# Writing the ranks into the first table with two half-size transfers, from SyncE and from ScalarE

## The chip, the cores and the metric

The kernel runs on one core of one Trainium2 chip. Times are device microseconds of that core. The kernel before took 3037.67 us (median of 3 runs, 3028.95 to 3050.73).

## What is computed

Four graph-attention layers run over one graph of 3327 nodes with 512 features a node. The adjacency is symmetric, has ones on its diagonal and is sparse (two nodes are joined with a probability of about 0.0048). Each layer normalises the rows, cuts them at zero, projects them, weighs the neighbours of each node by a softmax over them, and adds the mean to its input:

```python
h = jnp.maximum(_layernorm(x, axis=-1), 0.0)
x = x + layer(h, adj)                      # four times: 8, 4, 1 and 8 heads

# inside a layer, for each head
v = h @ W                                  # features
e = leaky_relu(s_target[:, None] + s_source[None, :], 0.2)
e = where(adj > 0, e, -inf)
out = softmax(e, axis=1) @ v               # elu after layers 1 and 2
```

## The kernel before

The nodes are padded to 3328 and cut into 26 tiles of 128 rows. There are two stages.

**First stage (`tile_gat_stack`, from L543).** For each tile of adjacency rows, GpSimd multiplies the row by descending keys (L695) and VectorE takes the largest 40 of them (L704, L659 to L661). That gives each node the list of its neighbours, in `L`. Beside this, the first layer's features are computed on TensorE, and for each node a row of 1056 numbers goes to the table `tabx` in DRAM (`features`, L684, on SyncE's queue): the features and scores of the source in the first half of the row, the node's own x and scores in the second. The rows of x come in on ScalarE's queue (L723).

The nodes are then ranked by the length of their lists, so that the 26 tiles of the second stage hold nodes with lists of like length (`CAPS` gives the length of each tile). `held` is the length of each node's list; `sorted_in` and `placed` count how many nodes come earlier. L735 to L739 add this up to `rank`, a tile of 128 x 26 numbers: column t holds the ranks of the nodes of tile t. From `rank` two things are made:

- L741 writes it to `tabx`, one number to each of the 3328 rows, in column `F // 2` = 256. It is one transfer on SyncE's queue. A node that gathers a neighbour's row so gets the neighbour's rank with it.
- L744 to L747 split it into `hi` (the tile) and `lo` (the place in the tile). With these, VectorE makes two sets of 0/1 masks and list copies (L765 to L782), and TensorE sorts the lists by rank by multiplying with the masks (L786). ScalarE copies the result to index tiles (L787, and doubled at L788), in two parts: part a holds the lists of tiles 18 to 25, part b those of tiles 1 to 17 and of tile 0.

One value, `bad`, tells whether the lists fit; the engines load it at L790 and branch. With these inputs the branch goes to `tile_gat_lists`.

**Second stage (`tile_gat_lists`, from L796).** The four layers go through the tiles in the order 25 to 0. For each tile, groups of up to four neighbours are fetched ahead (`fetch`, L857): GpSimd issues one indirect transfer for each neighbour (L835), which gathers 128 rows by one column of an index tile. In layer 0 it gathers from `tabx`. VectorE and ScalarE make the weights (`scored`, L876), VectorE multiplies (L917), and TensorE adds up (L922). In layer 0, ScalarE also takes the ranks out of the gathered rows (L894) and overwrites the indices with them, since the tables of the later layers (`tab0`, `tab1`) are written in the order of the ranks. Tiles of nodes with many neighbours are computed densely beside this in layers 1 to 3 (`Several`, `Wholes`).

**What sets the order.** Around the edit, GpSimd, TensorE, VectorE and ScalarE keep the order in which the program is written (`manual_schedule`, L732); SyncE's order is the scheduler's. Every engine starts its instructions in its own order. A transfer adds to one of eight completion counters, taken in turn by the transfers of SyncE and ScalarE, and who needs its data waits for that counter. The first gather, issued by GpSimd, so waits for the rows of `tabx`, for the ranks and for the indices.

Of the kernel before, what the change touches and what calls it, by code (L numbers as in the profile page):

```python
# [18 lines left out]
P = 128  # L19
# [505 lines left out]
def tile_gat_stack(ctx: ExitStack, tc: tile.TileContext, x, adj, adjT, ws, avs, out):  # L525
# [10 lines left out]
    nc = tc.nc  # L536
    NP, F = x.shape
    N = adjT.shape[0]
    NT = NP // P
# [5 lines left out]
    tabx = dram.tile([NP + 1, 2 * ROW], F32, name="tabx")  # L545
# [15 lines left out]
    with ExitStack() as c1:  # L561
# [170 lines left out]
        with tc.manual_schedule(engines={mybir.EngineType.Pool, mybir.EngineType.PE,  # L732
                                         mybir.EngineType.DVE, mybir.EngineType.Activation}):

            nc.vector.tensor_tensor_scan(base[:, 1:], ones[:, :BINS], count, 0.0, OP.mult, OP.add)  # L735
            nc.vector.tensor_mul(o, o, base[:, :BINS].unsqueeze(1).to_broadcast([P, NT, BINS]))
            rank = small.tile([P, NT], F32, name="rank", bufs=1)
            nc.vector.tensor_reduce(rank, o, AX.X, OP.add)
            nc.vector.tensor_add(rank, rank, part)  # L739

            nc.sync.dma_start(tabx[:NP, :].rearrange("(t p) c -> p t c", p=P)[:, :, F // 2:F // 2 + 1],  # L741
                              rank.unsqueeze(2))
            hi = small.tile([P, NT], F32, name="hi", bufs=1)
            nc.vector.tensor_scalar(hi, rank, 1.0 / P, -(P - 1) / 2.0 / P, OP.mult, OP.add)  # L744
            nc.vector.tensor_scalar(hi, hi, ROUND, -ROUND, OP.add, OP.add)
            lo = small.tile([P, NT], F32, name="lo", bufs=1)
            nc.vector.scalar_tensor_tensor(lo, hi, -float(P), rank, OP.mult, OP.add)  # L747

            junk = small.tile([P, BINS], F32, name="junk")
            nc.vector.tensor_tensor(junk, base[:, :BINS], limit, OP.is_gt)
            nc.vector.tensor_reduce(wrong[:, 2:3], junk, AX.X, OP.add)
            pn = ps_n.tile([P, BANK], F32, name="pn", bufs=1)
            nc.tensor.matmul(pn[0:1, :3], ones[:, 0:1], wrong, start=True, stop=True)
            worst = small.tile([1, 1], F32, name="worst", bufs=1)
            nc.vector.tensor_reduce(worst, pn[0:1, :3], AX.X, OP.max)
            nc.vector.tensor_copy(bad, worst)


            for i, part_ in enumerate(slots.parts):
                t0, t1 = min(b[0] for b in part_.blocks), max(b[1] for b in part_.blocks)
                high = fixed[:, 304:512] if i == 0 else ps_k.tile([P, BANK], F32, name="high")
                high = high[:, :NT * (t1 - t0)].rearrange("p (t h) -> p t h", h=t1 - t0)
                nc.vector.tensor_tensor(high, ahead[:, t0:t1].unsqueeze(1).to_broadcast([P, NT, t1 - t0]),  # L765
                                        hi.unsqueeze(2).to_broadcast([P, NT, t1 - t0]), OP.is_equal)
                n = part_.columns
                if i == 0:
                    (_, _, k, _), = part_.blocks
                    every = once.tile([P, NT, n], F32, name="every")  # L770
                    nc.vector.tensor_tensor(every.rearrange("p t (h k) -> p t h k", k=k),
                                            L[:, :, :k].unsqueeze(2).to_broadcast([P, NT, t1 - t0, k]),
                                            high.unsqueeze(3).to_broadcast([P, NT, t1 - t0, k]), OP.mult)
                pi = ps_i.tile([P, BANK], F32, name="pi")
                for t in range(NT):
                    if i == 0:
                        rhs = every[:, t, :]
                        nc.vector.tensor_scalar(low[:, t, :], ahead, lo[:, t:t + 1], None, OP.is_equal)
                    else:
                        rhs = spare[:, t % 2, :]  # L780
                        for b0, b1, k, c in part_.blocks:
                            nc.vector.tensor_tensor(  # L782
                                rhs[:, c:c + (b1 - b0) * k].rearrange("p (t k) -> p t k", k=k),
                                L[:, t, :k].unsqueeze(1).to_broadcast([P, b1 - b0, k]),
                                high[:, t, b0 - t0:b1 - t0].unsqueeze(2).to_broadcast([P, b1 - b0, k]), OP.mult)
                    nc.tensor.matmul(pi[:, :n], low[:, t, :], rhs, start=(t == 0), stop=(t == NT - 1))  # L786
                nc.scalar.activation(part_.idx, pi[:, :n], AF.Copy)  # L787
                nc.scalar.activation(part_.twice, pi[:, :n], AF.Copy, scale=2.0)  # L788
# [655 lines left out]
```

## Time and profile before

| | |
|---|---|
| median of 3 runs | 3037.67 us |
| the profiled execution | 2485.15 us |
| its span, first to last instruction | 2483.4 us |
| first stage, to `rank` | 0 to 259 us |
| from `rank` to the first gather | 259 to 273.5 us |
| layers 0 to 3 | 273.5 to 2483.4 us |
| VectorE busy, 0 to 259 / 259 to 273.5 | 215.54 / 13.29 us |
| ScalarE busy, 0 to 259 / 259 to 273.5 | 179.09 / 0.43 us |
| GpSimd busy, 0 to 259 / 259 to 273.5 | 210.26 / 0.04 us |

The profiled execution is one run and shorter by 552.5 us than the median of the others. Times in the views count from the span's start. A row of the timeline gives start, duration, engine, line, operation, what it writes and reads, and in brackets how long its engine had been idle before it and what ended that. "SPq" is the sequencer of SyncE, "POOLq" that of GpSimd; a transfer's row there is its issue, not its movement. The releaser in brackets is inferred.

### The profile page before, as it was taken

The page shows a single profiled execution, that of the slowest core. Times are in us where ns is not written, and L with a number is a line of the kernel's source. Part 1 is how long each engine was busy: PE and PEld are TensorE (multiplying, and loading weights), DVE is VectorE, ACT ScalarE, POOL GpSimd, SP SyncE. Part 2 cuts the span into 40 slices and gives each one's busy share as a digit, 9 for nine tenths or more (in the row PEclk, how much of TensorE's full clock was granted, in tenths as well). Part 3 has the DMA queues.
Part 4 walks back from the last instruction along what each step waited for, and adds up shares of the span by engine and source line. Part 5 has one row for each costly group of instructions (what it writes and reads, how often), then busy time and mean ns, then how long its engine had stood idle before and what let it go on. Part 6 is the DMA issues. An engine that isn't in the chain of part 4 may idle for free. (4 is left out here: it accounts for less than half of the span.)

```text
span 2483.4 us, 26799 instructions
## 1 busy us (share of the span) xinstructions
PE 2077.1 (84%) x6832; PEld 1161.7 (47%) x6832; DVE 1935.1 (78%) x5004; ACT 910.9 (37%) x2506; POOL 1709.5 (69%) x1700
## 2 busy tenths in 40 slices
PE   3778699999988846999999986869696699999897
PEld 1666345454444423555555543444353454455453
DVE  7988787887777725888888867978979488787776
ACT  4777024343321102434333323433333444333330
POOL 7898467777777756776777746655545377777775
PEclk9888899999999977999999998989898899999999
DMA  6796579999987878887888858867776488888885
GB/s 229 300 304 236 174 240 283 298 289 293 275 269 235 232 182 243 263 248 227 247 259 258 253 150 272 268 197 250 209 227 204 141 254 246 247 249 248 242 242 173
DMA packets 262490, 599.55 MB, mean 241 GB/s; under 512 B 103923, under 2 KB 121331, under 8 KB 257974
## 3 DMA queue, kind: packets, MB, share of 16 engines
q0 software_dynamic: 126128, 438.08, 58.6%
q1 hardware_dynamic: 132454, 152.86, 19.1%
q10 hardware_dynamic: 3744, 6.82, 0.8%
q8 instruction: 55, 0.90, 0.1%
q14 instruction: 109, 0.89, 0.1%
HBM read 547.96 MB, written 49.65 MB: 241 GB/s over the span
## 5 line engine op out<-in xcount | busy, mean ns | idle before, releaser
L922 PE MATMUL bank<-m,ident 128*128 128x512 f32 x2608 | 1202.3, 607 | 131.9 <-DVE m L917 131.2
L917 DVE TENSOR_TENSOR m<-g,pw 128x512 f32<-128x512 f32 x1304 | 810.7, 681 | 138.2 <-ACT pw L891 133.2
L835 POOL DMA_INDIRECT g<-tab,idxb x734 | 697.8, 951 | 281.7 <-issue 170.7
L922 PEld LDWEIGHTS bank<-m,ident 128*128 128x128 f32 x2608 | 482.7, 193 | 711.8 <-issue 345.2
L469 PE MATMUL pv<-w,hT 128*128 128x264 f32 x1664 | 439.0, 419 | 71.0 <-ACT hT L458 41.7
L891 ACT ACTIVATE pw<-z 128x32 f32<-128x32 f32 (+5 forms) x434 | 84.0, 194 | 987.8 <-DVE z L890 987.5
L469 PEld LDWEIGHTS pv<-w,hT 128*128 128x128 f32 x1664 | 336.5, 206 | 173.2 <-ACT hT L458 48.3
L835 POOL DMA_INDIRECT g<-tabx,twiceb x342 | 324.0, 947 | 104.4 <-issue 77.1
L835 POOL DMA_INDIRECT g<-tab,idxa x297 | 283.0, 953 | 148.0 <-issue 81.3
L1138 PE MATMUL whole<-ve,em 128*128 128x512 f32 x468 | 222.0, 623 | 41.0 <-DVE em L1124 38.9
L888 DVE TENSOR_TENSOR z<-g,pw 128x32 f32<-128x32 f32 (+5 forms) x434 | 75.0, 173 | 195.8 <-DMA g<-tab,idxa 88.4
L695 POOL TENSOR_TENSOR key<-a,keys 128x3328 int32<-128x3328 int32 (+1 forms) x29 | 189.4, 6536 | 16.6 <-DVE cand L704 12.9
L912 DVE SCALAR_TENSOR_TENSOR bank<-g,pw,bank 128x512 f32<-128x512 f32 x243 | 183.2, 754 | 6.8
L1138 PEld LDWEIGHTS whole<-ve,em 128*128 128x128 f32 x468 | 90.5, 199 | 151.1 <-issue 91.8
L704 DVE MAX8 cand<-key 128x8 f32<-128x208 int32 x416 | 143.8, 364 | 0.1
L835 POOL DMA_INDIRECT g<-tabx,twicea x99 | 94.4, 954 | 69.6 <-issue 31.3
L451 PE MATMUL pt<-ident,xn 128*128 128x128 f32 x416 | 68.8, 292 | 84.5 <-ACT hT L458 30.9
L451 PEld LDWEIGHTS pt<-ident,xn 128*128 128x128 f32 x416 | 54.3, 150 | 121.5 <-issue 49.4
L1113 ACT ACTIVATE r<-low,mc,b 128x384 f32<-128x384 f32 x78 | 52.6, 674 | 150.1 <-DVE em L1124 115.7
L1247 ACT ACTIVATE r<-low,spare 128x256 f32<-128x256 f32 x208 | 98.9, 476 | 5.1
L432 POOL TENSOR_TENSOR rstd<-ve,half 128x1 f32<-128x1 f32 x52 | 31.9, 615 | 94.8 <-DVE ve L975 60.4
L890 DVE SCALAR_TENSOR_TENSOR z<-z 128x32 f32<-128x32 f32 (+5 forms) x434 | 78.7, 181 | 15.2 <-DVE z L888 0.2
(175 smaller groups left out, 2113.6 us busy)
## 6 DMA issues: line engine op xcount, KB each, us to landing
a<-in_adj SPq DMA_DIRECT2D x25, 1664.0 KB
tab<-v SPq DMA_DIRECT2D x78, 264.0 KB
ve<-tab SPq DMA_DIRECT2D x78, 264.0 KB
g<-tab SPq DMA_DIRECT2D x66, 264.0 KB
tabx<-vx SPq DMA_DIRECT2D x26, 528.0 KB
g<-tab,idxb POOLq DMA_INDIRECT x734, 3.9
low<-tab SPq DMA_DIRECT2D x52, 132.0 KB
room<-tab SPq DMA_DIRECT2D x52, 132.0 KB
```

The source lines that it names most:

```text
L451: nc.tensor.transpose(pt[:, k, :], xn[:, k * P:(k + 1) * P], ident)
L469: nc.tensor.matmul(pv[:, s, :HF + 8], hT[:, k, :], W.w[:, k, s, :], start=(k == 0), stop=(k == KC - 1))
L695: nc.gpsimd.tensor_tensor(key[:, c:c + quarter], a[:, c:c + quarter], keys[:, c:c + quarter], OP.mult)
L704: nc.vector.max(cand[:, g * 8:(g + 1) * 8], key[:, g * SEG:(g + 1) * SEG])
L835: nc.gpsimd.indirect_dma_start(out=out_, out_offset=None, in_=table, in_offset=bass.IndirectOffsetOnAxis(ap=which, axis=0))
L890: nc.vector.scalar_tensor_tensor(z, z, SLOPE, z, OP.mult, OP.max)
L891: nc.scalar.activation(self.wt[:, k0:k0 + n, :H], z, AF.Exp)
L912: nc.vector.scalar_tensor_tensor(acc, v, w, acc, OP.mult, OP.add)
L917: nc.vector.tensor_tensor(m[:, q, :].rearrange("p (s h d) -> p s h d", s=2, d=D), v.rearrange("p s (h d) -> p s h d", d=D), wt[:, k0 + q, ...
L922: nc.tensor.matmul(self.po, ident, m[:, q, :], start=(k0 + q == 0), stop=(k0 + q == K - 1))
L1138: nc.tensor.matmul(tl.po.rearrange("p (s m) -> p s m", s=2), e[:, q * P:(q + 1) * P], v.rearrange("p (s m) -> p s m", s=2)[:, :, :F // 2], ...
L1247: nc.scalar.activation(self.r[:, h, :], self.a[:, g, :], AF.Relu, bias=-1.0, scale=self.b[:, j, g:g + 1])
```

## The change

The view of the 3328 places in `tabx` gets a name. The ranks of tiles 0 to 12 are written by a transfer on SyncE's queue, those of tiles 13 to 25 by one on ScalarE's queue. Each is of 128 x 13 numbers in place of 128 x 26. In the program the second stands between the copies of the last list (L630) and those of the first index part (L787 of before). Nothing else is edited. The lines after it move down by one.

```diff
             nc.vector.tensor_reduce(rank, o, AX.X, OP.add)
             nc.vector.tensor_add(rank, rank, part)
 
-            nc.sync.dma_start(tabx[:NP, :].rearrange("(t p) c -> p t c", p=P)[:, :, F // 2:F // 2 + 1],
-                              rank.unsqueeze(2))
+            places = tabx[:NP, :].rearrange("(t p) c -> p t c", p=P)[:, :, F // 2:F // 2 + 1]
+            nc.sync.dma_start(places[:, :NT // 2, :], rank[:, :NT // 2].unsqueeze(2))
+            nc.scalar.dma_start(places[:, NT // 2:, :], rank[:, NT // 2:].unsqueeze(2))
             hi = small.tile([P, NT], F32, name="hi", bufs=1)
             nc.vector.tensor_scalar(hi, rank, 1.0 / P, -(P - 1) / 2.0 / P, OP.mult, OP.add)
```

## The prediction

> **What bounds the kernel now.** I read the page's first part for the whole, then only the stretch in which the edited line runs, because a transfer of 13 KB can only matter where somebody waits for it. The page first:
>
> ```profile
> span 2483.4 us, 26799 instructions
> PE 2077.1 (84%) x6832; PEld 1161.7 (47%) x6832; DVE 1935.1 (78%) x5004; ACT 910.9 (37%) x2506; POOL 1709.5 (69%) x1700
> ```
>
> TensorE is busy for 84% of the span, VectorE for 78%, GpSimd for 69%: over the whole no single engine is the bound. The edited line runs once, at 258.86 us, between the two large stages: before it the edge lists are sorted (VectorE 215.5 us of the first 259.0), after it the four layers run. So the question is local: which wait ends last in front of the first gather, the first instruction that reads what the edited line writes? The timeline from 258 us on, with start, duration, engine, line and the idle time before:
>
> ```profile
> 258.65 0.19 DVE L739 TENSOR_TENSOR rank<-rank,part 128x26 f32<-128x26 f32 x1
> 258.86 0.37 SPq L741 DMA_DIRECT2D tabx<-rank  x1
> ...
> 260.76 3.40 DVE L771 TENSOR_TENSOR every<-L,fixed 128x3120 f32<-128x3120 f32 x1
> 264.08 6.80 DVE L778 TENSOR_SCALAR low<-fixed,lo 128x128 f32<-128x128 f32 x26
> ...
> 264.48 8.08 PE L786 MATMUL pi<-every,low 128*128 128x120 f32 x52 [4.41 <-DVE low L778]
> ...
> 272.59 0.27 ACT L787 ACTIVATE idxa<-pi 128x120 int32<-128x120 f32 x1 [18.34 <-PE pi L786]
> 272.76 0.27 ACT L788 ACTIVATE twicea<-pi 128x120 int32<-128x120 f32 x1
> ...
> 273.46 1.19 POOL L835 DMA_INDIRECT g<-tabx,twicea  x1 [29.15 <-DMA av<-in_a]
> ```
>
> Two branches leave `rank` at 258.84 us. One is the transfer. The other makes the gather's indices: VectorE to 270.88, TensorE to 272.56, ScalarE to 273.03. The gather starts at 273.46, 0.43 us after the index tile is finished, and cannot start earlier whatever the transfer does. The page names a load of `av` as the releaser; that load was issued at 267.27 and the gather neither reads nor overwrites it, so I take the label as an inference from a shared completion counter. GpSimd's own semaphore instructions in front of that gather say the same more directly (durations are min/median/max in ns):
>
> ```profile
> L835 POOLq EVENT_SEMAPHORE  x5: 17/43/6863, 265.4 to 265.7; - x5
> ```
>
> The long one starts at 265.7 and ends 6.863 us later, at 272.56: that is TensorE's end (264.48 + 8.08). Everything else that GpSimd waited for there was already done. When did the transfer land? The DMA view of the queues (packets, MB, share of the 16 engines), cut to 258.5 to 265 us:
>
> ```profile
> q1 hardware_dynamic: 3344, 0.01, 25.7%
> ```
>
> and cut to the one us from 260:
>
> ```profile
> q1 hardware_dynamic: 1701, 0.01, 75.6%
> ```
>
> 3344 packets on SyncE's queue are 26 x 128 = 3328 ranks and 16 more, and in the second us the 16 DMA engines were busy to 75.6%. Cutting the view finer, the first packets come in 259 to 260 us and the last at about 262.24. So the transfer takes 262.24 - 258.86 = 3.4 us, and its cover is 273.46 - 262.24 = 11.2 us.
>
> **What the Trainium skill says.** "DMA: Bandwidth & Descriptors", section "Rules for kernel authors": a DMA whose last dimension is not contiguous becomes one descriptor for each element. The trace agrees (3344 packets for 3328 elements). The same page, "Why a DMA increments its semaphore by 16 and not by 1": each engine in use posts its own completion, 16 for a transfer over 128 partitions; 3344 - 3328 = 16 agrees. The same page, "Issuing engines are not separate DMA queues": transfers started by different engines run on the same 16 DMA engines and interleave, so a second issuer saves only the sequencer's time. The trace of before has no such pair; the 75.6% says that little is left to gain. "Perfetto Trace Analysis", "DMA Instruction — HWDGE (DVE, Sync)": the profiled window of such an instruction is its issue, not the movement; 0.37 us against 3.4 us agrees.
>
> **The change part by part.**
>
> *SyncE's issue, now of 13 tiles.* One issue of 0.37 us stays, for 1664 elements in place of 3328. If it shrinks with the number, it saves up to 0.19 us. SyncE then loads the branch flag at 260.5 and next issues at 265.71, in the other branch. Worth 0.
>
> *ScalarE's issue, added.* The row to price it by is ScalarE's loads of x (L723): 334 ns median, 957 ns at most. In the built program it stands behind L630, which starts at 254.01 and lasts 0.24, and ahead of L787 at 272.59; it waits for `rank` (258.84) and for five DMA counters of earlier row writes. Before, SyncE's issue waited for those same five counters, and it started 0.02 us after `rank`, so they are no later. It should start near 258.9 and end before 259.9. Behind it on ScalarE are L787 and L788, on which the gather waits, and they wait for TensorE until 272.56: 12.7 us of ScalarE's idle time (18.34 in all) cover an issue of 0.33 to 0.96. Worth 0; without that cover up to 1 us.
>
> *The movement.* 3328 data packets stay and completions go from 16 to 32: 3360 packets. From 1701 packets in one us, 16 more cost about 0.01 us. If the two queues fill the engines from 75.6% to 100%, the 3344 packets, which take some 2.5 us of movement, end 0.6 us sooner. If the queues do not overlap at all, the second half starts after the first: a second 0.8 us of latency between issue and first packet (258.86 to about 259.7), so 0.8 us later. The landing moves between -0.8 (with the saved issue) and +0.8 us, and I take -0.3. All of it is under the 11.2 us of cover, so the value for the end is 0 at both ends. With the cover gone it would be that same -0.8 to +0.8.
>
> *Waits.* The first gather has one counter more to wait for. GpSimd's semaphore instructions there take 17 ns at least and 43 at the median, and they run from 265.4, ahead of the long wait for TensorE: 0, without cover 0.05. Every later transfer of SyncE and ScalarE moves on by one of eight completion counters. I compared the built orders: PE, DVE and GpSimd issue the same instructions in the same order, ScalarE has one more, SyncE's later order is the same, and once counters are renumbered, the waits in the layers that run are unchanged but for one additional one at the first products of layer 0 (VectorE L917, at 302.20) and one fewer on ScalarE's copy of x; the additional one is for a transfer landed 40 us before. Worth 0.
>
> Sum: 0 + 0 + 0 + 0 = 0 us against the profiled execution, 2485.15 us (span 2483.4 and 1.75 around it). The runs shown have a median of 3037.67, 552.5 us more than the profiled execution; this profile does not show where that goes, so I carry the sum over as it is: 3037.7 us. For the transfer to matter in those runs, it would have to lose 11.2 us of cover.
>
> **The rivals.**
>
> *The wait really is for the transfer (faster).* In the longer runs the single-element writes might be much slower than in this trace, and the gather wait for them. At best the two issuers halve the transfer. To gain over 1%, 30.4 us, it would have to take over 61 us in place of 3.4, about 18 times as long. For it: 552 us are unexplained, and the page puts the 29.15 us of idle time down to a DMA. Against: the semaphore row above, and the shared 16 engines. At 70 us halved it gives 3037.7 - 35 = 3003 us.
>
> *The half on ScalarE's queue lands late (slower).* The place is the first gather, with all of layer 0 behind it. Each us past 273.46 costs at most one us. It decides from 11.2 us of delay on; to lose 1% it must land 30.4 us after 273.46, at 303.9, so 45 us after an issue at 258.9. Even an issue put off until behind L788 (273.03) would land at 276.4 and cost 3.0 us, 0.1%. 45 us for 1664/16 = 104 packets an engine is 0.43 us a packet, where 1701 packets in one us over 16 engines are 9.4 ns a packet. Nothing in the profile is near. At 40 us past, 3078 us.
>
> *The change doesn't do what it says.* The two transfers run after one another on the engines and land when the one did, or 0.8 us later. It can well be, and it gives the same 3037.7 us, so I count it with the forecast.
>
> **How the numbers follow.** Hidden, whether the landing moves or not: 0.90. Faster through the transfer: 0.04. Slower through ScalarE's queue: 0.04. The remaining 0.02 is for things I haven't named, half to each side. About 1% is what a measurement of this kernel can tell from no change: so 0.05 faster, 0.90 the same, 0.05 slower. The three runs shown spread over 3050.73 - 3028.95 = 21.8 us; I take that spread to either side, 3015.9 to 3059.5, and about 4 us more for the costs above without their cover (3.0 of a late issue and 0.8 of transfer): 3012 to 3064. The rivals lie outside it, with less than 2 in 10.
>
> **What would show it.** Right: two issues at about 258.9, one on SyncE and one on ScalarE; 3360 small packets, the last between 261.4 and 263.1; L787 near 272.6 and the first gather near 273.5, still 0.4 us after the index; span within 1% of 2483. Wrong: the first gather more than 1 us after L788's end, L787 idle for another reason than TensorE, or small packets after 273 us. If the time moves by over 1% and the first gather stays where it is, the cause lies outside everything I have priced.

## The result and the profile after

The changed kernel took 3028.65 us (median of 22 runs, 3001.95 to 3055.61), the kernel before 3030.21 us (22 runs, 3015.63 to 3050.73). The ratio is 0.9995, with a 95% interval of 0.9974 to 1.0015: no change. The forecast was 3037.7 us, which is the old median of 3 runs carried over, and a change of 0.

The page of the changed kernel begins:

```profile
span 3026.3 us, 26802 instructions
PE 2238.7 (74%) x6832; PEld 1226.8 (41%) x6832; DVE 1931.8 (64%) x5004; ACT 913.5 (30%) x2506; POOL 1713.8 (57%) x1700
```

The two profiled executions must not be compared over the whole: 3026.3 us here, 2483.4 us before, with the same work (VectorE is busy for 1931.8 and 1935.1 us). The runs further down were made on three chips. On two of them the kernel before takes 2485 to 2487 us, at a granted TensorE clock of 0.94; on the third one run of it took 3041.78 us at 0.87. The two profiles here have clocks of 0.944 and 0.867, so I take them to come from different chips; which ones is not known. The stretch up to the first gather is alike on all chips (`rank` is done between 256.5 and 259.1 us), so that stretch can be compared. The changed kernel's timeline there:

```profile
258.58 0.19 DVE L739 TENSOR_TENSOR rank<-rank,part 128x26 f32<-128x26 f32 x1
258.79 0.37 SPq L742 DMA_DIRECT2D tabx<-rank  x1
258.80 0.45 ACTq L743 DMA_DIRECT2D tabx<-rank  x1
...
264.41 8.93 PE L787 MATMUL pi<-every,low 128*128 128x120 f32 x52 [4.41 <-DVE low L779]
...
273.38 0.27 ACT L788 ACTIVATE idxa<-pi 128x120 int32<-128x120 f32 x1 [19.88 <-PE pi L787]
273.55 0.26 ACT L789 ACTIVATE twicea<-pi 128x120 int32<-128x120 f32 x1
...
274.25 1.19 POOL L836 DMA_INDIRECT g<-tabx,twicea  x1 [30.70 <-DMA w<-in_w]
```

Both halves are issued within 0.03 us of `rank`, one on each queue. The gather starts 0.44 us behind the doubled index (273.81), where it was 0.43 us before. It is 15.48 us behind `rank`, where it was 14.62, and TensorE's product accounts for that: 8.93 us, where it was 8.08. GpSimd's semaphore instructions ahead of the gather again end with TensorE, whose last product is done at 273.34; the long wait starts at 265.8 and lasts 7.556 us:

```profile
L836 POOLq EVENT_SEMAPHORE  x5: 17/43/7556, 265.5 to 265.8; - x5
```

The DMA view of the changed kernel, cut to 258.5 to 265 us (q1 is SyncE's queue, q10 ScalarE's):

```profile
q10 hardware_dynamic: 1680, 0.01, 11.9%
q1 hardware_dynamic: 1680, 0.01, 11.5%
```

and cut to the one us from 260:

```profile
q1 hardware_dynamic: 1272, 0.01, 56.7%
q10 hardware_dynamic: 418, 0.00, 18.3%
```

There are 3360 packets, 32 of them completions. In the us from 260 both queues together moved 1272 + 418 = 1690 packets, where the one queue had moved 1701. The shares differ because SyncE's first packet came at 259.95 and ScalarE's at 260.39. Where both are under way, from 260.7 to 261.2, they share evenly:

```profile
q10 hardware_dynamic: 427, 0.00, 37.4%
q1 hardware_dynamic: 422, 0.00, 36.9%
```

That is 849 packets in half a us. The kernel before, with its one queue, moved 850 from 260.5 to 261:

```profile
q1 hardware_dynamic: 850, 0.00, 75.0%
```

The second queue took its packets from the first one's share. The last packet left at about 262.05, 3.26 us after the issue (3.38 before). The landing is later than that: by the trace's semaphore records the last of the sixteen completions came at 265.58 in the kernel before, 6.72 us after its issue, and in the changed one at 265.67, 6.87 us after.

One more thing can be read ahead of the gather. In each of the thirteen profiles it starts 0.84 to 0.86 us after the last of GpSimd's semaphore instructions, also where the index had been ready for several us. ScalarE needs 0.47 us after TensorE's last product for the two index copies, so these end inside that time. What holds the gather, then, is TensorE's product, from which the index is made; the 0.43 us behind the doubled index are what is left of the 0.86.

### The profile page after: what moved, and what is told of

Same layout as the page of the kernel before. It is cut to its first block, busy times and chain, and to the rows that moved or that the text cites. A ratio compares the mean times of both kernels' runs of the same rounds, so it can differ in the third digit from the quotient of the medians.

```text
span 3026.3 us, 26802 instructions
## 1 busy us (share of the span) xinstructions
PE 2238.7 (74%) x6832; PEld 1226.8 (41%) x6832; DVE 1931.8 (64%) x5004; ACT 913.5 (30%) x2506; POOL 1713.8 (57%) x1700
## 5 line engine op out<-in xcount | busy, mean ns | idle before, releaser
L923 PE MATMUL bank<-m,ident 128*128 128x512 f32 x2608 | 1316.6, 653 | 359.3 <-DVE m L918 234.8
L923 PEld LDWEIGHTS bank<-m,ident 128*128 128x128 f32 x2608 | 524.7, 209 | 1014.5 <-issue 608.0
L1139 PE MATMUL whole<-ve,em 128*128 128x512 f32 x468 | 233.9, 651 | 48.5 <-DVE em L1125 15.1
L476 ACT ACTIVATE v<-pv,rstd 128x528 f32<-128x528 f32 x78 | 54.2, 695 | 316.0 <-remote 183.1
L1259 ACT ACTIVATE spare<-room,low 128x64 f32<-128x64 f32 x208 | 59.1, 337 | 195.8 <-remote 69.4
L1248 ACT ACTIVATE r<-low,spare 128x256 f32<-128x256 f32 x208 | 98.9, 476 | 14.1 <-remote 5.0
L458 ACT ACTIVATE hT<-pt 128x512 f32<-128x512 f32 x104 | 61.3, 589 | 132.1 <-PE pt L451 56.3
```

The lines of the kernel that those rows point to most:

```text
L923: nc.tensor.matmul(self.po, ident, m[:, q, :], start=(k0 + q == 0), stop=(k0 + q == K - 1))
L1139: nc.tensor.matmul(tl.po.rearrange("p (s m) -> p s m", s=2), e[:, q * P:(q + 1) * P], v.rearrange("p (s m) -> p s m", s=2)[:, :, :F // 2], ...
L1248: nc.scalar.activation(self.r[:, h, :], self.a[:, g, :], AF.Relu, bias=-1.0, scale=self.b[:, j, g:g + 1])
L1259: nc.scalar.activation(vs[:, h, :D], self.v[u % 3][:, h * D:(h + 1) * D], AF.Copy, scale=c[:, h:h + 1])
```

## The experiments

The theory on trial: the first gather waits for the index, and the transfer has some us of cover. The rival: the gather waits for the transfer, and two queues merely failed to shorten it. In all of these runs, time is counted from `rank` (the end of L739), since from one run to the next the first stage ends at 256.5 to 259.1 us (later only in the run without the transfer).

### The kernel before once more

No edit; it asks whether the distance between the two profiles belongs to the edit.

> The kernel before, unedited, in one more profiled execution. The first profiled execution of it had a span of 2483.4 us, that of the changed kernel 3026.3, while the medians of 22 runs of each are equal (3030.21 and 3028.65). Theory: the difference between the two profiles is none of the edit's, and this execution lies near 3030 us, with the first stage as before (rank at 258.8, first gather at 273.5 to 274.3) and all of the difference after 280 us, at a lower granted clock. Rival: the kernel before has a profile of 2483 us again, and the medians hide something that the edit does.

Its span was 2482.5 us, and 15 runs of the kernel before on that chip have a median of 2484.74 us. So the kernel before has a profile of 2483 us again, against what I expected; the medians hid no effect of the edit, as the next run shows.

### The changed kernel once more

No edit either; on a chip whose runs scatter less.

> The changed kernel, unedited, beside the kernel before on one chip, since the runs before this one came from a chip where 15 runs of the kernel before lie within 0.4% of each other. Theory: ratio 0.998 to 1.002; the first gather 14.1 to 14.7 us behind rank, 0.4 us behind the doubled index, as in the kernel before. Rival (the two transfers do something that the wider spread of the first comparison hid): a ratio outside that, with the first gather moved.

2485.57 us against 2487.41 (14 and 35 runs): ratio 0.9996, interval 0.9984 to 1.0007. The expectation for the time held. That for the gather did not: it came 15.64 us behind `rank`, not 14.1 to 14.7. TensorE's product took 9.09 us here. The same product took 7.60 to 9.10 us over all profiles, and about 9.0 also where one queue alone is used (8.97 with the transfer three times, 9.10 with one half late); between 259 and 273.5 us the granted clock was 0.58 in this run, 0.60 in the first profile of the changed kernel, 0.66 and 0.69 in the two of the kernel before. The gather still starts 0.43 us behind the doubled index. So this delay is TensorE's and not the transfer's.

### The transfer three times, and twenty times

```diff
-            nc.sync.dma_start(tabx[:NP, :].rearrange("(t p) c -> p t c", p=P)[:, :, F // 2:F // 2 + 1],
-                              rank.unsqueeze(2))
+            places = tabx[:NP, :].rearrange("(t p) c -> p t c", p=P)[:, :, F // 2:F // 2 + 1]
+            for _ in range(3):                     # or 20
+                nc.sync.dma_start(places, rank.unsqueeze(2))
```

> The whole transfer from SyncE, three times in a row, each behind the landing of the one before. Theory (the gather waits for the index, the transfer has 11 us of cover): the third lands near 258.9 + 3 x 3.4 = 269.1, still ahead of the index, and the first gather stays 0.4 us behind L788, at 273.5 to 274.3. Rival (the gather waits for the transfer): the first gather starts about 6.8 us later than before, near 280.

The timeline of this run:

```profile
257.62 11.67 SPq L743 DMA_DIRECT2D tabx<-rank  x3
...
272.40 0.27 ACT L789 ACTIVATE twicea<-pi 128x120 int32<-128x120 f32 x1
...
275.76 1.19 POOL L836 DMA_INDIRECT g<-tabx,twicea  x1 [33.39 <-PE pi L787]
```

and GpSimd's semaphore instructions in it:

```profile
L836 POOLq EVENT_SEMAPHORE  x5: 17/43/10556, 264.0 to 274.9; - x5
```

Neither expectation was met. The three issues start 5.65 us apart ((11.67 - 0.37) / 2), not 3.4, so the third was issued at 268.92. The index was ready at 272.67, but the gather started 3.09 us later, and GpSimd was free of its last wait at 274.9: this time it did wait for the transfer. The gather waits for the later of the two. That wait is the one for the third transfer's completion counter: it ended at 274.65, and the transfer had landed at 274.62. My 3.4 us were the time to the last packet, not the time until the waiting engine sees the landing. The end did not move: 2485.30 us in one run, against 2484.74.

> The whole transfer twenty times in a row, so that it outlasts its cover. Theory: the last one lands near 258.9 + 20 x 3.4 = 327, the first gather starts there, 53 us late, and the end moves by 20 to 55 us (ratio 1.007 to 1.018): less than 53 where VectorE, which is busy with the second index part until 295 or later, would not have started layer 0 at once. Rival (nothing in layer 0 waits for the ranks in time): first gather at 274, ratio 1.000.

The queue's own times to landing in this run, and the first gather in its timeline:

```profile
DMA to landing us min/median/max: 5.6/5.9/6.1
```

```profile
374.97 1.19 POOL L836 DMA_INDIRECT g<-tabx,twicea  x1 [132.73 <-SPq L1440]
```

The last of the twenty landed 116.3 us after the first issue (about 5.8 us for each), and the gather started 117.51 us behind `rank` (257.46). That is 102.9 us later than the 14.62 of before. The time was 2577.44 us against 2484.74: ratio 1.0378 (1.0362 to 1.0394), 92.7 us more. I had expected at most 55, by the same mistake of 3.4 for 5.9. Past the cover nearly every us of the transfer is paid at the end, but not every one. The profiled execution, the shortest of the four, took 2573.06 us, 88.3 us more than before. VectorE's first instruction on gathered data shows why:

```profile
386.10 0.17 DVE L887 COPY pw<-g 128x8 f32<-128x8 f32 x1 [86.54 <-DMA g<-tabx,idxa]
```

VectorE stood idle for 86.54 us until the gather had landed, and that is about what the execution lost. The other 16 us of the 102.9 were hidden behind VectorE's earlier work.

### No transfer

```diff
-            nc.sync.dma_start(tabx[:NP, :].rearrange("(t p) c -> p t c", p=P)[:, :, F // 2:F // 2 + 1],
-                              rank.unsqueeze(2))
...
+            nc.scalar.activation(vx[:, F // 2:F // 2 + 1], own[:, t:t + 1], AF.Copy)
             nc.sync.dma_start(tabx[t * P:(t + 1) * P, :], vx)
```

> The transfer is left out. Each node's own number is put in the place of its rank by a small ScalarE copy for each tile of the first stage (26 of about 0.2 us, beside other work), so that layers 1 to 3 take rows in another order than they should. Theory: the first gather stays 0.4 us behind the doubled index, at 273.5 to 275, and the time is within 0.3% of before (ratio 0.997 to 1.003). Rival (the gather waits for the transfer, and two queues only failed to make it shorter): the first gather comes earlier than the index tile plus 0.4 us allows in the kernel before, and the ratio is under 0.997.

2491.88 us against 2484.74 (11 and 15 runs): ratio 1.0022, interval 1.0011 to 1.0032. `own`, the nodes' own numbers, is made at the first tile for this. The added copies on ScalarE put `rank` itself back to 266.45, 7.6 us later than in the first profile, and so the gather came at 280.61 and not by 275; the 7.1 us of the ratio are of that size. Behind `rank` the gather came after 14.16 us, and the second profile of the kernel before has 14.15. With no transfer at all to wait for, the gather is not earlier.

### The cover taken away: the whole, the pair, a half, a quarter

The transfer at the old place is taken out. ScalarE copies `rank` behind the doubled index, and the transfer takes the copy. Then the index no longer hides it from the gather, and the time from its issue to the gather is its own, but for some 1.1 us that GpSimd needs after the landing.

```diff
-            nc.sync.dma_start(tabx[:NP, :].rearrange("(t p) c -> p t c", p=P)[:, :, F // 2:F // 2 + 1],
-                              rank.unsqueeze(2))
...
                 nc.scalar.activation(part_.twice, pi[:, :n], AF.Copy, scale=2.0)
+                if i == 0:
+                    late = small.tile([P, NT], F32, name="late", bufs=1)
+                    nc.scalar.activation(late, rank, AF.Copy)
+                    places = tabx[:NP, :].rearrange("(t p) c -> p t c", p=P)[:, :, F // 2:F // 2 + 1]
+                    nc.sync.dma_start(places, late.unsqueeze(2))
```

> The kernel before with the cover taken away: ScalarE copies rank behind the doubled index of the first part (273.0), and the one transfer on SyncE takes its numbers from that copy, so that the first gather can only wait for the transfer. It measures the transfer by itself. The chain of twenty showed 5.6 to 6.1 us from one issue to the landing that the next waits for, so the first gather should start 5.8 to 7 us after the issue, near 280, and the end move by at most 7 us (0.3%).

```profile
270.90 0.37 SPq L791 DMA_DIRECT2D tabx<-late  x1
...
277.96 1.19 POOL L838 DMA_INDIRECT g<-tabx,twicea  x1 [35.91 <-PE pi L784]
```

7.06 us from the issue to the gather; the queue's time to landing was 6.0. The pair has this in place of the last line:

```diff
+                    nc.sync.dma_start(places[:, :NT // 2, :], late[:, :NT // 2].unsqueeze(2))
+                    nc.scalar.dma_start(places[:, NT // 2:, :], late[:, NT // 2:].unsqueeze(2))
```

> As late_whole, with the two transfers of 13 tiles from SyncE and ScalarE in place of the one of 26. It measures the edit with nothing to hide it. Theory (the packets, not the issuers, set the time, at about 1690 a us in both kernels): from issue to the first gather the same as in late_whole within 0.4 us. Rival (two queues halve the movement of 2.5 us): at least 1 us less than in late_whole.

```profile
271.84 0.37 SPq L791 DMA_DIRECT2D tabx<-late  x1
271.85 0.45 ACTq L792 DMA_DIRECT2D tabx<-late  x1
...
278.62 1.19 POOL L839 DMA_INDIRECT g<-tabx,twicea  x1 [36.20 <-SPq L1443]
```

6.78 us: 0.28 us less than the whole, within the 0.4 that the theory allowed. One run of each doesn't show that the edit is worth 0.28 us. By the semaphore records one whole transfer took from 5.5 to 6.7 us to land over these runs, and the pair 5.7 us here, but 6.9 and 6.1 in the two profiles of the changed kernel, where the kernel before had 6.7 and 5.8. What the runs show is that the pair isn't faster by anything near the 1 us of the rival. Two more runs send only a part late; the other ranks are written at the old place:

```diff
+            nc.sync.dma_start(places[:, NT // 2:, :], rank[:, NT // 2:].unsqueeze(2))
...
+                    nc.sync.dma_start(places[:, :NT // 2, :], late[:, :NT // 2].unsqueeze(2))
```

> As late_whole, but only tiles 0 to 12 wait behind the index; the ranks of tiles 13 to 25 are written at the old place, from SyncE, and are landed long before. It measures one transfer of half the size with nothing beside it. In late_whole it was 7.06 us from the issue to the first gather, in late_pair 6.78. If the 2.5 us of movement scale with the packets and the rest is fixed, one half takes 7.06 - 1.25 = 5.8 us. That is what the pair would have taken if its two queues moved at full rate side by side. If the pair's time is fixed cost instead, one half takes 6.8 as well.

4.57 us (issue at 273.18, gather at 277.75), less than either 5.8 or 6.8. A half beside nothing is 2.49 us shorter than the whole, though the packets alone would give 1.25. The part after the last packet shrinks too, from about 3.7 us to about 2.7; without GpSimd's 1.1 us that is 2.6 and 1.4 us up to the landing. Alone, SyncE's half landed 3.4 us after its issue; in the pair it took 4.7 and ScalarE's 5.7, so the two halves hold each other up. So I took a price for each written number up to its landing, and tried it on a smaller part: the same edit with 6 in place of `NT // 2`.

> As late_one_half, but only tiles 0 to 5 (768 numbers) wait behind the index; the ranks of the other 20 tiles are written at the old place. From the issue to the first gather it took 7.06 us for 3328 numbers and 4.57 for 1664: 1.5 ns for each number and 2.1 us besides. Theory (every single-element write has its price up to the landing, whichever queue it comes from, which is why the pair saved 0.28 us only): 2.1 + 768 x 0.0015 = 3.2 us, 3.0 to 3.5. Rival (the part behind the last packet, 3.7 us for the whole and 2.7 for the half, stops shrinking): 0.8 + 0.6 + 2.7 = 4.1 us or more.

3.37 us (272.14 to 275.51), within the expected 3.0 to 3.5 and under the rival's 4.1. From 768 to 1664 numbers each costs 1.34 ns more, from 1664 to 3328 1.50 ns; each of these times is from one run, so the price is a rough one. This run came from the third chip: 3037.83 us against 3041.78 for the kernel before beside it.

The late kernels show no longer time, though their gathers come later: 2484.08 us (whole) and 2482.92 us (pair), where the kernel before ran from 2481.06 to 2494.05 us, and 2486.52 us (one half) against 2485.14, one run each. What covers them is seen on VectorE. Its first instruction on gathered data, in the second profile of the kernel before and then with the whole transfer late:

```profile
299.87 0.16 DVE L886 COPY pw<-g 128x8 f32<-128x8 f32 x1
```

```profile
299.06 0.16 DVE L889 COPY pw<-g 128x8 f32<-128x8 f32 x1
```

Neither row has a wait in brackets. Behind `rank` (259.08 and 256.45) they are 40.79 and 42.61 us, while the gather is 14.15 and 21.51 us behind it. The changed kernel, whose gather was not held by its transfer, has 42.01 us in its second profile, so the 1.82 us between the two can't be put down to the late gather. Until 294 to 296 us VectorE makes the list copies for the second index part, and it takes up layer 0 some 4 to 5 us later. By the semaphore records the gather that this row reads had landed at 281.08 in the kernel before and at 289.60 with the transfer late, over 9 us ahead of it. The first gathers only have to be early enough for that.

### SyncE and GpSimd

As the late pair, with `nc.gpsimd` in place of `nc.scalar`.

> As late_pair, with the second half issued by GpSimd, [...]in place of ScalarE. It asks what sets the rate of about 1700 packets a us, at which SyncE and ScalarE together moved no more than SyncE alone. Theory 1 (the 16 DMA engines or the memory set it): both queues together stay under 1750 packets a us wherever they overlap. Theory 2 (SyncE and ScalarE share what makes their descriptors): over 2000 a us where they overlap. The gather itself comes later than in late_pair if GpSimd takes longer to make 1664 descriptors than the others.

It does not tell the two theories apart: GpSimd's half went out as 48 packets in place of 1664 and more (16 of 256 bytes, 16 of 160 and the 16 completions, so 64 and 40 numbers to a packet), after SyncE's were done, so there was no overlap in which to count. From SyncE's issue (270.85) to the gather (277.66) it took 6.81 us, near the pair's 6.78. GpSimd's half landed 5.5 us after its issue and SyncE's 3.7 after its own.

### ScalarE alone

```diff
-            nc.sync.dma_start(tabx[:NP, :].rearrange("(t p) c -> p t c", p=P)[:, :, F // 2:F // 2 + 1],
+            nc.scalar.dma_start(tabx[:NP, :].rearrange("(t p) c -> p t c", p=P)[:, :, F // 2:F // 2 + 1],
```

> The kernel before with its one transfer issued by ScalarE in place of SyncE. Theory: the issue of 0.4 to 1 us lies in ScalarE's idle time between L630 and L787, the index is not later, the first gather stays 14.1 to 14.7 us behind rank, ratio 0.998 to 1.002. Rival (an issue on ScalarE's queue, or its landing, is late enough to hold the index or the gather): the gather more than 15 us behind rank, with ScalarE's copies of the index later than TensorE's end.

2485.93 us against 2487.41 (20 and 35 runs): ratio 0.9993, interval 0.9986 to 1.0000. The issue took 0.39 us, and the gather came 14.49 us behind `rank` (256.79 to 271.28). The expectation held.

## Why the prediction was right

**The wait that ends last.** Shown: the first gather waits for the index, by way of TensorE's product. It starts 0.43 to 0.44 us behind the doubled index in the kernel before, in the changed one, and where there is no transfer to wait for, and only with the transfer late does it start later.

**The issue on ScalarE.** Forecast 0.33 to 0.96 us, near 258.9; measured 0.45 us at 258.80, with 14 us of idle time behind it. Worth nothing, as forecast.

**The movement.** Of -0.8 to +0.8 us I took -0.3, and the one comparison without cover gave -0.28. That they agree is luck: with cover, the pair landed 0.15 and 0.3 us later than the one transfer in the two profiles of each kernel, and single transfers scatter by more. The reason was only partly right. I let the two queues fill the engines from 75.6% up to 100%. They did not: 1690 packets a us, where it had been 1701, and 849 in half a us where it had been 850. Nor did they start as one queue does: with both issues within 0.01 us, SyncE's first packet came 1.16 us and ScalarE's 1.59 us after the issue, in three profiles, where a transfer by itself had its first packet after 0.9 to 1.0 us (I had 0.8). The late half and quarter say why there is little to gain: some 1.3 to 1.5 ns for each number up to its landing, and the pair writes as many numbers as the whole. Which part sets that price, the DMA engines or the memory behind them, no run separates.

**The cover.** This is the term that was mis-sized. I took the last packet as the landing: 3.4 us, and 11.2 us of cover. What a waiting engine sees is the completion: the transfer of the kernel before landed at 265.58, and GpSimd's last wait, for TensorE, ended at 272.60, so the cover was 7.0 us. The page "Perfetto Trace Analysis" of the Trainium skill, section "DMA Instruction — HWDGE (DVE, Sync)", says that the last descriptor waits until the write before it is confirmed and that this can take long for a target in HBM; the late whole agrees, with about 2.6 us from its last packet to the landing. I had read it for the issue alone. For the same reason an issue put off until behind the index was priced at 3.0 us for the gather; the late pair's gather came 6.92 us behind the doubled index in place of 0.43, so 6.5 us late. On the other side I left out a cover: behind the gather lies VectorE's work on the second index part, which hid that delay (one run) and some 16 us of the 102.9 of the twenty transfers. Both errors left the sum at 0.

**The rival of a faster kernel** fell with the three transfers and with none. **The rival of a slower one** had its price right: at most one us for each us late; measured 92.7 for 102.9. Its point of decision was put on the gather, and is later, by VectorE's cover.

**The 552.5 us** that I carried over without a cause go with the chip, as far as the runs tell: every execution of the kernel before or of the changed one on two chips lies between 2479.94 and 2494.59 us, and the two executions on the third, of the kernel before and of the late quarter, near 3040. On the slower one the stretch to the first gather is as on the others, and the layers are longer, at a clock of 0.87 in place of 0.94. The clock differs by 8% and the time by 22%; where the rest is from was not tried.

## What to carry to other kernels

Before a transfer is split or moved to another queue, find who waits for it and what else that waiter needs: here the index was later than the ranks, and the whole transfer could be left out without the gather coming earlier. Read a transfer's landing from a consumer that has nothing else to wait for, not from its last packet; for the whole transfer here the two differ by 2.1 to 3.3 us. Then follow the delay on to the engine that is busy behind the consumer: here a gather 7 us late was not felt. A second queue brought nothing that could be told from the scatter here, where the cost goes with the number of single-element writes.

## What the runs showed of the hardware

- A transfer of 3328 single four-byte numbers to DRAM landed 5.5 to 6.7 us after its issue, while the last packet left after 3.0 to 3.6 us.
- Two queues under way together were served evenly and no faster than one: 427 and 422 packets in half a us, where one queue alone moved 850.
- Two transfers issued within 0.01 us on SyncE and ScalarE had their first packets 1.16 and 1.59 us after the issue; by itself, the whole transfer's came after 0.93 us from SyncE and 0.96 from ScalarE.
- GpSimd's queue carried 1664 single-element writes as 48 packets in the record, where SyncE's had 1680; packets of the two kinds of queue can't be compared by number.
- GpSimd's indirect transfer started 0.84 to 0.86 us after the last semaphore instruction ahead of it, in all thirteen profiles.
- The kernel before took about 2485 us on two chips and 3041.78 us on a third, and the first stage took about as long on each: `rank` was done at 259.1 us on one of the two, and at 257.8 us on the third (there in the late quarter).
